# Copies of x to the output: issued one by one inside the experts' tiles instead of all ahead of the first expert weights

## The chip, the cores and the metric

The kernel runs as one program on one core of a Trainium2 chip. The metric is the device time of one execution in microseconds (us), lower is better. The time before is 1151.77 us, the median of 3 runs (1147.62 to 1153.18). The core has five engines, each with an instruction queue of its own that it works off strictly in order: PE (TensorE, matrix products), DVE (VectorE, elementwise and reductions), ACT (ScalarE, functions and copies), POOL (GpSimd, here mostly issuing indirect transfers) and SP (SyncE, issuing DMA transfers). Transfers run on 16 DMA engines that all issuers share.

## The reference

```python
xn = layernorm(x)                          # x: 8 x 512 x 256, f32
# recurrent attention, 16 heads of 16, for each token:
S = S * exp(gk)[..., None]
sab = einsum('bhk,bhkv->bhv', a, S)
S = S + k[..., None] * (sab[..., None, :] + v[..., None, :])
o_t = einsum('bhk,bhkv->bhv', q, S)
s = layernorm(o * sigmoid(xn @ Wog1 @ Wog2)) * norm_w @ Wo
# mixture of experts, 8 experts, the best 2 for each token:
for e in range(8):
    moe += cw[:, e] * (gelu(xn @ W1[e] + b1[e]) @ W2[e] + b2[e])
out = x + s * silu(layernorm(moe) * gamma + beta)
```

x has 4096 tokens of 256 numbers, W1 of an expert is 256 x 1024 and W2 1024 x 256, so that the weights of one expert are 2 MB.

## The kernel before

**Stages and chunks.** The 512 steps of a sequence are cut into 8 stages of 64 steps. Within a stage the recurrence is solved in closed form over chunks (of 16 or 8 steps, in turns by stage), so that the state S is renewed 48 times in all: chunks c0 to c47. The chain of chunks is the serial backbone. In a chunk PE first multiplies the state with the stage's tables (`by_state`, matmul L898), DVE makes `RO` of it (L929), PE multiplies `RO` with the keys `KT` (`by_keys`, L963), ACT decays the state (L908), and DVE renews it (`S`, L975). The tables FA and KT of a stage are made ahead by `fine(s)` and `solve`, which are long runs of DVE work (lines 713 to 816); `output` (L1026, L1035) makes the stage's output, also on DVE. `fetch(s)` (L651) loads a stage's projected queries, keys and decays from memory as `raw` (L654), and `turn_keys` has ACT copy them to `X` (L666), with which the stage's DVE work begins.

**Experts.** `experts` works through 39 tiles of sorted token rows, t0 to t38: 32 tiles of 256 rows (two pieces of 128) and 7 half tiles of 128 rows, 71 pieces in all. For a tile, `load_weights` (L1063 to L1069) issues 2 transfers of 1 MB on SP (w1 at L1066, w2 at L1068), one tile ahead; `load_rows` gathers rows on POOL (L1078); `turn` transposes them (L1091). PE then makes `ph` (L1122, 16 matmuls, in four groups, each followed by a Gelu on ACT, L1130), and `py` (L1143, 8 matmuls for a piece); ACT scales it to `y` (L1151), and POOL adds it to the sums in memory by an indirect transfer (`y_dram`, L1099). The trace records each of these matmuls twice, so 16 matmuls are 32 records.

**Attention's end and the finish.** For each stage, `attend(s)` loads `by_state` and `o_f` on SP, adds them (DVE, L1206), gates them with a sigmoid of `p2` (PE L1213, ACT L1217, DVE L1220), takes moments (L1164) and normalizes (ACT, L1177), transposes on PE (`pz`, L1234), and multiplies with Wo (`po`, L1241). The buffers behind `by_state`, the gate and the transposed copy are one and the same, single (tag `t_f`), and so is `o_f`, so that the stages follow one another here. When the last tile is done, `fetch_sums` reads the sums of all stages back on POOL (L1268), and `finish(s)` takes moments of them (DVE, L1164), normalizes, applies gamma, beta and SiLU, multiplies with the attention's part, and adds the product to the output in memory (an accumulating transfer on POOL). The output must hold x by then: 16 copies of 256 KB (8 stages x 2 halves, L1370) move it there from memory to memory, issued on SP by `everything_else` just before `experts` starts, in build order. `behind(instruction, now["spread"])` only pins such an instruction's place behind another one in the schedule.

**What sets the order.** The program is built by generators that `yield` estimated costs. `stretch(s)` goes through the chunks of a stage, and at set points of each chunk `both` spends credit on three lists: `inner` (the DVE work of `recurrence`), `between` (`attend`) and `beside` (sorting, projections, `experts`, `finish`). What `beside` gets at a chunk is `per_chunk` = (`beside_cost` - what is spent) / (chunks left + 4), so `beside_cost` (L1428) sets how soon the experts' tiles are placed among the chunks. The tiles that are left when the chunks are over come after them, mixed with the last stages of `attend`. Each engine then runs its instructions in the order in which they were so placed.

Of the kernel before, what the change touches and what calls it, by code (L numbers as in the profile page):

```python
# [30 lines left out]
def recurrent_attn_moe_kernel(  # L31
# [23 lines left out]
    nc = tc.nc  # L55
# [5 lines left out]
    NF = DFF // P  # L61
    NTB = T // NB
    NP = B * NB // P
# [15 lines left out]
    def bank(name):  # L79
        return ps_p.tile([P, 512], F32, tag="ps", name=name)  # L80
# [61 lines left out]
    for i in range(2):  # L142
        t = sp.tile([P, GC, 2 * D], F32, name=f"vz{i}", bufs=1)
# [5 lines left out]
    def rows_of(ap, s, bb):  # L149

        return ap.rearrange("(c bb) t d -> bb t c d", bb=2)[bb, s * NB : (s + 1) * NB]

    made, now = {}, {}
# [484 lines left out]
    def behind(ins, first):  # L638

        tc.add_manual_dep(  # L640
            ins.ins,
            first.ins.name,
            mybir.DependencyInfo(mybir.DependencyClass.NoSync, mybir.DependencyReason.DATA),
            reason="what it waits for has that long",
        )
# [416 lines left out]
    def experts(mp):  # L1062
        def load_weights(t):  # L1063
            e = nc.sync.value_load(owner[0:1, t : t + 1], min_val=0, max_val=E - 1)
            w1 = mp.tile([P, KD, DFF], F32, name="w1")
            nc.sync.dma_start(w1, W1[bass.ds(e, 1)].rearrange("o (j p) f -> p (o j) f", p=P))  # L1066
            w2 = mp.tile([P, NF, D], F32, name="w2")
            nc.sync.dma_start(w2, W2[bass.ds(e, 1)].rearrange("o (f p) d -> p (o f) d", p=P))  # L1068
            return w1, w2  # L1069

        def pieces(t):

            return range(2 * t, 2 * t + 2) if t < NXW else (NXW + t,)

        def load_rows(t):
            xs = mp.tile([P, TS // P, D], F32, name="xs", bufs=4)
            for n, r in enumerate(pieces(t)):
                nc.gpsimd.indirect_dma_start(  # L1078
                    out=xs[:, n],
                    out_offset=None,  # L1080
                    in_=xn_dram[:, :],
                    in_offset=bass.IndirectOffsetOnAxis(ap=source[:, r : r + 1], axis=0),
                )
            return xs

        def turn(t, xs):
            size = len(pieces(t))
            pt = bank("pt").rearrange("p (j t) -> p j t", j=KD)
            for j in range(KD):
                for n in range(size):  # L1090
                    nc.tensor.transpose(  # L1091
                        pt[:, j, n * P : (n + 1) * P], xs[:, n, j * P : (j + 1) * P], ident
                    )
            xT = mp.tile([P, KD, TS], F32, name="xT_s")
            nc.scalar.copy(xT[:, :, : size * P], pt[:, :, : size * P])
            return xT

        def add_to_sums(r, y):
            nc.gpsimd.indirect_dma_start(  # L1099
                out=y_dram[:, :],  # L1100
                out_offset=bass.IndirectOffsetOnAxis(
                    ap=target[:, r : r + 1], axis=0
                ),
                in_=y,
                in_offset=None,
                compute_op=ALU.add,
            )

        now_xs, nxt = load_rows(0), load_rows(1)
        w1, w2 = load_weights(0)  # L1110
        xT = turn(0, now_xs)
        yield 0.9
        for t in range(NX):
            size = len(pieces(t)) * P
            hs = []
            for f in range(0, NF, 2):
                ph = bank("ph").rearrange("p (k t) -> p k t", k=2)
                h = mp.tile([P, 2, TS], F32, name="h", bufs=6)
                hs.append(h)
                for k in range(2):  # L1120
                    for j in range(KD):
                        nc.tensor.matmul(  # L1122
                            ph[:, k, :size],
                            w1[:, j, (f + k) * P : (f + k + 1) * P],
                            xT[:, j, :size],
                            start=(j == 0),
                            stop=(j == KD - 1),
                        )
                for k in range(2):
                    nc.scalar.activation(  # L1130
                        h[:, k, :size], ph[:, k, :size], AF.Gelu, bias=bias[:, t, f + k : f + k + 1]
                    )
                if f == 0:
                    now_xs, nxt = nxt, load_rows(t + 2) if t + 2 < NX else None
                    ahead = load_weights(t + 1) if t + 1 < NX else None
                yield 1.9
            if t + 1 < NX:
                xT = turn(t + 1, now_xs)
                yield 0.9
            for n, r in enumerate(pieces(t)):  # L1140
                py = bank("py")[:, :D]
                for f in range(NF):
                    nc.tensor.matmul(  # L1143
                        py,
                        hs[f // 2][:, f % 2, n * P : (n + 1) * P],
                        w2[:, f],
                        start=(f == 0),
                        stop=(f == NF - 1),
                    )
                y = mp.tile([P, D], F32, name="y", bufs=4)  # L1150
                nc.scalar.activation(y, py, AF.Identity, scale=weight[:, r : r + 1])  # L1151
                add_to_sums(r, y)
                if n == 0 and size == TS:
                    yield 3.9
            if ahead:
                w1, w2 = ahead
            yield 3.9

    experts_cost = NXW * (4 * 1.9 + 0.9 + 2 * 3.9) + NXH * (4 * 1.9 + 0.9 + 3.9)
# [106 lines left out]
    def fetch_sums(fp, s):  # L1266
        g = fp.tile([P, NP, D], F32, name="g", bufs=NTB)
        nc.gpsimd.dma_start(  # L1268
            g,
            y_dram[s * NP * P : (s + 1) * NP * P].rearrange("(n p) d -> p n d", p=P),  # L1270
        )
        return g

    def finish(fp, s, g):
        mv = fp.tile([P, NP, 2], F32, name="mv_g", bufs=4)
        for i in range(NP):
            moments(fp, g[:, i], i, mv)
        yield 2.5
        r = yield from deviation(fp, mv)
        for i in range(NP):  # L1280
            normed(g[:, i], i, r)
        yield 1.0
        wide = [P, NP, D]
        nc.vector.tensor_tensor(g, g, now["gam"].unsqueeze(1).to_broadcast(wide), ALU.mult)
        yield 1.2
        nc.vector.tensor_tensor(g, g, now["bet"].unsqueeze(1).to_broadcast(wide), ALU.add)
        nc.scalar.activation(g, g, AF.Silu)
        yield 1.2
        if s in LATE:
            gated[s] = g  # L1290
            return
        while s not in attended:
            yield WAIT
        att = fp.tile([P, NP, D], F32, name="att_f", bufs=3)
        nc.gpsimd.dma_start(att, att_d[s].rearrange("n p d -> p n d"))
        yield 1.0
        nc.vector.tensor_tensor(g, g, att, ALU.mult)  # L1297
        yield 1.2
        for bb in range(2):
            nc.gpsimd.dma_start(  # L1300
                rows_of(out, s, bb), g[bb * NB : (bb + 1) * NB], accum_op=ALU.add
            )
# [56 lines left out]
    def everything_else():  # L1359

        for s in range(2, NTB):
            yield from project(s, xT_all[:, s])
        while not cp:
            yield WAIT
        projecting.close()
        prologue.close()

        for s in range(NTB):
            for bb in range(2):
                behind(nc.sync.dma_start(rows_of(out, s, bb), rows_of(x, s, bb)), now["spread"])  # L1370
            yield 0.2
        with tc.tile_pool(name="moe", bufs=2, side="right") as mp:
            yield from experts(mp)
        fp = late.enter_context(tc.tile_pool(name="fin", bufs=2, side="right"))
        for name, ap in (("gam", gamma), ("bet", beta)):
            now[name] = fp.tile([P, D], F32, name=f"{name}_sb", bufs=1)
            nc.sync.dma_start(now[name], ap.partition_broadcast(P))
        sums = [fetch_sums(fp, s) for s in range(NTB)]
        yield 1.0
        for s in range(NTB):  # L1380
            beside.queue.append(finish(fp, s, sums[s]))
# [43 lines left out]
        cost = fine_cost(s + 1) if s + 1 < NTB else 0.0  # L1425
        return cost + output_cost(s - 1) if s else cost

    beside_cost = experts_cost + (NTB - 2) * NP * 2 * 1.8 + 16 * 0.8 + 8 * 0.5 + 64 * 0.7 + 10 + NTB * 0.4  # L1428

    def stretch(s):  # L1430
        C = CS[s]
# [84 lines left out]
```

## Time and profile before

| what | value |
|---|---|
| median of 3 runs | 1151.77 us |
| profiled execution | 1149.24 us, of which the span 1147.4 us |
| mean granted TensorE clock | 0.883 |
| PE busy | 894.6 us (78%) |
| DVE busy | 878.1 us (77%) |
| ACT busy | 688.0 us (60%) |
| POOL busy | 355.6 us (31%) |
| memory traffic | 196 GB/s over the span |

No engine is busy all the time, and the shares are means over very different stretches. Until about 250 us the kernel projects, sorts and prepares; from there to about 1010 us it works through the chunks with the experts' tiles among them; then come the tiles that are left, and the finish.

How rows of the timeline are read: start (us from the start of the span), time, engine, line, operation, tiles (written <- read), shape, number of records; in brackets the time that the engine stood idle before, and the releaser that ended it.

### The profile page before, as it was taken

The numbers are of one execution on the slowest core, as the hardware profiler recorded it, in microseconds if no ns is written. First come the engines' busy times: TensorE is split into PE (matmuls) and PEld (weight loads), VectorE is DVE, ScalarE is ACT, GpSimd is POOL, SyncE is SP. The second block draws the span as 40 slices with busy tenths as digits, with TensorE's granted clock in tenths as the row PEclk, the third lists the DMA queues.
The fourth block names the chain that finished last, engine by engine and source line by source line (L and its number), as shares of the span: only waits on it lengthen the run. The fifth ranks groups of instructions, "written<-read, shape, count | busy, mean of one in ns | idle before, by whom it ended". The sixth has DMA issues, their size and how long they took to land. (4 is left out here: it accounts for less than half of the span.)

```text
span 1147.4 us, 24978 instructions
## 1 busy us (share of the span) xinstructions
PE 894.6 (78%) x9448; PEld 684.9 (60%) x9448; DVE 878.1 (77%) x1761; ACT 688.0 (60%) x1687; POOL 355.6 (31%) x312
## 2 busy tenths in 40 slices
PE   5979778619989869978899798679799889785312
PEld 2534354417778658856687577568587667684301
DVE  7579995959999695579999975999999546313494
ACT  3566566854456847665658478248765645434385
POOL 2300000132344323323446323244642134220334
PEclk9989888958999989998899889789899989997666
DMA  8777578689578976997499899477599987894786
GB/s 224 190 177 194 147 213 135 184 290 217 170 165 252 180 221 143 259 221 187 120 278 137 252 170 241 141 159 247 176 191 225 182 201 226 143 241 126 225 182 103
DMA packets 393255, 221.87 MB, mean 193 GB/s; under 512 B 280912, under 2 KB 362704, under 8 KB 392112
## 3 DMA queue, kind: packets, MB, share of 16 engines
q1 hardware_dynamic: 363248, 172.17, 60.6%
q0 software_dynamic: 25280, 43.93, 18.3%
q10 hardware_dynamic: 4608, 4.20, 1.5%
q8 instruction: 74, 1.21, 0.4%
q14 instruction: 45, 0.37, 0.1%
HBM read 152.07 MB, written 72.35 MB: 196 GB/s over the span
## 5 line engine op out<-in xcount | busy, mean ns | idle before, releaser
L1122 PE MATMUL ph<-xT_s,w 128*128 128x256 f32 (+1 forms) x1248 | 291.0, 390 | 16.3 <-DMA w<-in_L_ffn_W_dram 9.0
L1143 PE MATMUL py<-w,h 128*128 128x256 f32 x1136 | 275.8, 398 | 8.6 <-ACT h L1130 8.1
L1122 PEld LDWEIGHTS ph<-xT_s,w 128*128 128x128 f32 x1248 | 234.6, 206 | 53.1 <-issue 11.0
L1143 PEld LDWEIGHTS py<-w,h 128*128 128x128 f32 x1136 | 221.0, 200 | 46.0 <-ACT h L1130 12.9
L908 ACT ACTIVATE sdec<-S,PcF 128x64 f32<-128x64 f32 x752 | 189.6, 340 | 90.9 <-DVE S L975 82.0
L1099 POOL DMA_INDIRECT y_dram<-y,target x71 | 139.2, 1960 | 291.6 <-ACT y L1151 149.3
L1078 POOL DMA_INDIRECT xs<-xn_dram,source x71 | 116.9, 1646 | 343.1 <-DVE source L536 169.7
L1130 ACT ACTIVATE h<-ph,bias 128x256 f32<-128x256 f32 (+1 forms) x312 | 121.4, 450 | 79.6 <-PE ph L1122 78.6
L975 DVE SCALAR_TENSOR_TENSOR S<-PC,heads,sdec 128x256 f32<-128x256 f32 x188 | 78.9, 481 | 51.6 <-PE PC L963 43.4
L1151 ACT ACTIVATE y<-py,weight 128x256 f32<-128x256 f32 x71 | 33.1, 468 | 90.0 <-PE py L1143 89.9
L898 PE MATMUL PC<-S,FA 64*16 64x64 f32 (+1 forms) x3072 | 43.5, 234 | 50.2 <-DVE S L975 49.9
L963 PE MATMUL PC<-RO,KT 8*64 8x64 f32 (+1 forms) x3008 | 49.3, 242 | 35.8 <-DVE RO L929 20.8
L963 PEld LDWEIGHTS PC<-RO,KT 8*64 8x64 f32 (+1 forms) x3008 | 41.1, 139 | 55.2 <-DVE RO L929 25.5
L898 PEld LDWEIGHTS PC<-S,FA 64*16 64x16 f32 (+1 forms) x3072 | 34.3, 100 | 65.5 <-DVE S L975 55.6
L808 DVE TENSOR_TENSOR scratch_a<-Z,A 128x1020 f32<-128x1020 f32 (+21 forms) x88 | 67.8, 771 | 5.3 <-ACT fq L772 4.4
L733 DVE TENSOR_TENSOR scratch_q<-Z,X 128x64 f32<-128x64 f32 (+11 forms) x96 | 70.5, 734 | 0.0
L746 DVE TENSOR_REDUCE Z<-scratch_q 128x4 f32<-128x64 f32 (+11 forms) x96 | 70.1, 730 | 0.0
L816 DVE TENSOR_TENSOR Z<-Z,scratch_a 128x1020 f32<-128x1020 f32 (+21 forms) x88 | 67.6, 768 | 1.0
L1234 PE MATMUL pz<-ident,o_f 128*128 128x128 f32 x64 | 13.0, 334 | 61.9 <-ACT o_f L1177 61.4
L750 DVE TENSOR_TENSOR Z<-Z,X 128x64 f32<-128x64 f32 (+10 forms) x88 | 60.6, 688 | 0.1
L733 DVE TENSOR_TENSOR scratch_a<-Z,X 128x64 f32<-128x64 f32 (+10 forms) x88 | 60.5, 688 | 0.0
L746 DVE TENSOR_REDUCE A<-scratch_a 128x4 f32<-128x64 f32 (+10 forms) x88 | 60.3, 685 | 0.0
(227 smaller groups left out, 1366.0 us busy)
## 6 DMA issues: line engine op xcount, KB each, us to landing
w<-in_L_ffn_W_dram SPq DMA_DIRECT2D x78, 1024.0 KB
kqd<-st_p SPq DMA_DIRECT2D x48, 256.0 KB
raw<-kqd SPq DMA_DIRECT2D x8, 1536.0 KB
fq<-fq SPq DMA_DIRECT2D x8, 1024.0 KB
xn_dram<-xn SPq DMA_DIRECT2D x8, 512.0 KB
v<-st_p ACTq DMA_DIRECT2D x32, 128.0 KB
y_dram<-st_b SPq DMA_DIRECT2D x16, 256.0 KB
kt<-Z SPq DMA_DIRECT2D x8, 512.0 KB
```

The lines of the kernel that those rows point to most:

```text
L733: nc.vector.tensor_tensor(pr, Z[:, :, :upto, C:], step[:, m, i].unsqueeze(2).to_broadcast([P, n, upto, HD]), ALU.mult,)
L746: now["work"] = nc.vector.tensor_reduce(to, pr, AX.X, ALU.add)
L808: nc.vector.tensor_tensor(pr, Z[:, :, l, l:].unsqueeze(2).to_broadcast([P, n, l, w]), A[:, :, l, :l].unsqueeze(3).to_broadcast([P, n, l, w ...
L898: nc.tensor.matmul(p1[32 * q : 32 * q + 2 * C, b, m], FA[lo : lo + SB, 4 * q + m, c], S[lo : lo + SB, q, m], start=True, stop=True,)
L908: nc.scalar.activation(dec[:, n // 4, n % 4], S[:, n // 4, n % 4], AF.Copy, scale=PcF[:, n, c : c + 1])
L963: nc.tensor.matmul(p4[b * SB : (b + 1) * SB, q, m], KT[32 * q : 32 * q + C, lo : lo + SB], ro[32 * q : 32 * q + C, lo : lo + SB], start=Tr ...
L975: nc.vector.scalar_tensor_tensor(S.rearrange(flat)[:, :, at], p4.rearrange(flat)[:, :, at], heads[:, h : h + 1], now["dec"].rearrange(flat ...
L1078: nc.gpsimd.indirect_dma_start(out=xs[:, n], out_offset=None, in_=xn_dram[:, :], in_offset=bass.IndirectOffsetOnAxis(ap=source[:, r : r + ...
L1099: nc.gpsimd.indirect_dma_start(out=y_dram[:, :], out_offset=bass.IndirectOffsetOnAxis(ap=target[:, r : r + 1], axis=0), in_=y, in_offset=None,
L1122: nc.tensor.matmul(ph[:, k, :size], w1[:, j, (f + k) * P : (f + k + 1) * P], xT[:, j, :size], start=(j == 0), stop=(j == KD - 1),)
L1130: nc.scalar.activation(h[:, k, :size], ph[:, k, :size], AF.Gelu, bias=bias[:, t, f + k : f + k + 1])
L1143: nc.tensor.matmul(py, hs[f // 2][:, f % 2, n * P : (n + 1) * P], w2[:, f], start=(f == 0), stop=(f == NF - 1),)
```

## The change

The 16 copies are no longer issued together ahead of `experts`, but in the loop over a tile's groups: at the third of the four `ph` groups of the odd tiles t = 1, 3, ... 31, one copy each on SP, without `behind`. The planner's cost `beside_cost` is altered too: its second term was (8 - 2) x 4 x 2 x 1.8 = 86.4 and is now (8 - 2) x 7 x 1.8 = 75.6, and the last term, 8 x 0.4 = 3.2, is gone; so 769.6 became 755.6, of which the experts' own cost is 608.4.

```diff
--- before.py
+++ after.py
@@ -1130,6 +1130,10 @@
                     nc.scalar.activation(
                         h[:, k, :size], ph[:, k, :size], AF.Gelu, bias=bias[:, t, f + k : f + k + 1]
                     )
+                if f == NF // 2 and t % 2 and t // 2 < 2 * NTB:
+
+                    copy = t // 2 // 2, t // 2 % 2
+                    nc.sync.dma_start(rows_of(out, *copy), rows_of(x, *copy))
                 if f == 0:
                     now_xs, nxt = nxt, load_rows(t + 2) if t + 2 < NX else None
                     ahead = load_weights(t + 1) if t + 1 < NX else None
@@ -1364,11 +1368,6 @@
             yield WAIT
         projecting.close()
         prologue.close()
-
-        for s in range(NTB):
-            for bb in range(2):
-                behind(nc.sync.dma_start(rows_of(out, s, bb), rows_of(x, s, bb)), now["spread"])
-            yield 0.2
         with tc.tile_pool(name="moe", bufs=2, side="right") as mp:
             yield from experts(mp)
         fp = late.enter_context(tc.tile_pool(name="fin", bufs=2, side="right"))
@@ -1425,7 +1424,7 @@
         cost = fine_cost(s + 1) if s + 1 < NTB else 0.0
         return cost + output_cost(s - 1) if s else cost
 
-    beside_cost = experts_cost + (NTB - 2) * NP * 2 * 1.8 + 16 * 0.8 + 8 * 0.5 + 64 * 0.7 + 10 + NTB * 0.4
+    beside_cost = experts_cost + (NTB - 2) * 7 * 1.8 + 16 * 0.8 + 8 * 0.5 + 64 * 0.7 + 10
 
     def stretch(s):
         C = CS[s]
```

## The prediction

> **What bounds the kernel now.** I read three views of the profile: busy time by stretches, then the timeline around the first weights, where the change acts, then the timeline of the tail. The stretches first (length, busy time of PE, PE's weight loads, DVE, ACT and POOL, then granted clock, share of the DMA engines, GB/s):
>
> ```profile
> 245.00:440.00 195.00, 162.20 (x2129) 133.82 (x2130) 175.83 (x297) 113.70 (x305) 61.96 (x54) 0.90 0.82 202
> 440.00:500.00 60.00, 55.39 (x676) 46.32 (x676) 26.39 (x55) 44.50 (x110) 19.53 (x17) 0.98 1.02 209
> 500.00:640.00 140.00, 125.03 (x1609) 102.16 (x1608) 138.18 (x246) 89.50 (x239) 65.42 (x42) 0.91 0.77 187
> ...
> 900.00:1010.00 110.00, 89.50 (x1327) 74.72 (x1326) 53.33 (x136) 54.07 (x185) 35.96 (x27) 0.91 0.91 190
> 1010.00:1082.00 72.00, 42.82 (x243) 36.72 (x241) 15.48 (x52) 28.21 (x59) 16.85 (x19) 0.80 0.67 168
> 1082.00:1148.00 66.00, 15.25 (x56) 10.94 (x56) 46.56 (x120) 42.44 (x70) 24.34 (x25) 0.60 0.78 167
> ```
>
> See the DVE column: 175.83 of 195 us at 245 to 440 and 138.18 of 140 at 500 to 640, above PE's 162.20 and 125.03; so the stage work of DVE sets the pace there and PE has room. At 440 to 500 and 900 to 1010 it is PE. From 1010 on nobody is full: that is a chain of waits. Now the start:
>
> ```profile
> 209.37 8.61 SPq L1370 DMA_DIRECT2D out_dram<-in_L_attn_x_dram  x9
> ...
> 233.08 1.54 SPq L654 DMA_DIRECT2D raw<-kqd  x1
> ...
> 237.48 12.02 SPq L1370 DMA_DIRECT2D out_dram<-in_L_attn_x_dram  x7
> ...
> 245.48 5.62 ACT L666 COPY X<-raw 128x1024 f32<-128x1024 f32 x3 [10.12 <-DMA raw<-kqd]
> 245.69 1.18 PE L963 MATMUL PC<-RO,KT 16*64 16x64 f32 x52 [8.19 <-DMA KT<-kt]
> 249.29 0.20 DVE L713 COPY dec<-X 128x64 f32<-128x64 f32 x1 [10.69 <-ACT X L666]
> 249.72 0.43 SPq L1066 DMA_DIRECT2D w<-in_L_ffn_W_dram  x1
> ...
> 258.96 8.67 PE L1122 MATMUL ph<-xT_s,w 128*128 128x256 f32 x32
> ```
>
> Seven of the copies keep SP until 249.5 us, and the first weights go out at 249.72. PE has little from 237 to 259. But `ph` has no bracket: when PE reached it, straight behind chunk 1's L963, the weights were there; not they, but its place in PE's order kept it. The tail:
>
> ```profile
> 1060.08 2.84 PE L1122 MATMUL ph<-xT_s,w 128*128 128x128 f32 x24
> ...
> 1063.91 3.72 PE L1143 MATMUL py<-w,h 128*128 128x256 f32 x16
> ...
> 1068.42 1.58 POOL L1099 DMA_INDIRECT y_dram<-y,target  x1 [6.37 <-DMA by_state<-ro]
> 1073.25 1.23 DVE L1206 TENSOR_TENSOR o_f<-o_f,by_state 128x1024 f32<-128x1024 f32 x1 [21.62 <-DMA og<-og]
> 1074.24 1.63 POOL L1268 DMA_DIRECT2D g<-y_dram  x2 [4.23 <-DMA y_dram<-y,target]
> ...
> 1082.26 0.75 DVE L1164 BATCH_NORM_STATS2 st_f<-g 128x6 f32<-128x256 f32 x2 [3.62 <-DMA g<-y_dram]
> ...
> 1085.08 2.17 PE L1234 MATMUL pz<-ident,o_f 128*128 128x128 f32 x8 [17.44 <-ACT o_f L1177]
> ```
>
> The last tile's `py` ends at 1067.6, its scatter starts at 1068.42, the sums are read back from 1074.24, DVE has them at 1082.26, and the finish takes 1147.4 - 1082.26 = 65.1 us more. Stage 6 of `attend` (L1206 at 1073.25, `pz` at 1085.08) lies beside this and keeps nobody.
>
> **The change, part by part.** (1) The copies. In the order of the changed build, 7 still stand on SP ahead of the first weights (they depend on nothing and nothing holds them), among the last projections' stores; 9 come at later tiles. Issue: nine at 8.61/9 = 0.96 us at most, 8.6 us of SP spread over some 500 us, where SP only runs ahead. As bytes: 9 x 256 KB = 2.36 MB, read and written, at the page's mean 193 GB/s 12.2 us of a moved load whose total is the same, at stretches where the DMA share is 0.77 to 1.02. Behind each copy on SP stand the weights of a later tile, and KT loads. Bounds 0 and +12; I take +1, because a tile's weights go out a whole tile ahead.
>
> (2) The first weights go out ahead of `raw` and the KT loads of stage 0, at about 217 (where the nine copies' issue ended, 209.37 + 8.61 = 218.0). Tile 0 then stands on PE between chunk 0's L898 and L963, and tile 1 begins at chunk 1. A whole tile is 2 x (291.0 + 275.8)/71 = 16.0 us of PE, from the costly groups' busy times over 71 pieces. Most of it falls in PE's hole (8.19 us at 245.69 alone, 8.16 more ahead of chunk 1). Bounds for the chain: -16, if the tile is carried through as time, and +4, if it stands in front of chunk 0's L963. In favour of nothing: the renewals from 253 to 446 are paced by DVE (first row). I added, for each span between two renewals, the DVE work and the PE work that each build places in it, by these durations. From c0 to c12 the larger one sums to 186.4 us before and 181.0 after (192.9 real), from c12 to c16 63.1 and 64.5, c16 to c24 125.2 and 121.9, c24 to c29 97.6 and 94.0, c29 to c38 136.2 and 142.8, c38 to c46 91.9 and 95.5; in all 700.4 and 699.7. What PE gains early it gives back from c29 on. So the last renewal moves by -0.7; real time is 751.7, so 51.3 us are waits of other kinds, and I put +-7 on it.
>
> (3) `raw` of stage 2. It reached ACT 12.4 us after its issue (233.08 to 245.48), with seven copies right behind it; the other stages' took 7.1 to 19.3. Without the copies it can come 5.3 us sooner, or, behind 3 MB of weights now ahead of it, 6.9 later. DVE's idle 10.69 us ends there. Bounds -5.3 and +6.9; I take 0.
>
> The Trainium skill bears on (2) and (3) ("DMA: Bandwidth & Descriptors", section "Queues, rings and completion order"): on each DMA engine the descriptors of one issuer's ring are taken in order. By it the first weights would stand behind every copy that was issued before them, and taking nine away would free them by the 12.2 us that was worked out above. By the row, `ph` at 258.96 waits for no weights. By the rule taken as time, my total would be 12 us less, 1161; I follow the row. Against any gain speaks the same page's section "Issuing engines are not separate DMA queues": all transfers share 16 engines, so that a copy moved is still carried.
>
> (4) The planner. 14.0 less in `beside_cost` lowers `per_chunk` in each chunk, so that the experts fall behind. In the build's order, 35.5 tiles of `ph` and 67 pieces of `py` stand ahead of c47 before, and 34.5 and 66 after: one half tile more in the tail. That alone is 32 `ph` records at 2.84/24 us, 3.8, and 16 `py` records, 3.72: +7.5 us.
>
> (5) But the tail's order changes with it. `attend` is placed on its own credit, and so slides by one half tile against the experts. Before, stage 6's transposes `pz` stand behind the last tile. After, PE's order at the last tile is: 4 `ph` matmuls, half of `pz` of stage 6, 8 `ph`, the other half, 4 `po`, 4 `ph`, 8 `py`. So 12 of the 16 `ph` and all `py` of the last tile queue behind a wait for stage 6 to be normalized. Its L1206 starts at 1073.25, on transfers issued on SP when stage 5 freed `t_f`, which nothing here moves. From there by the rows: the gate product at 1075.63 takes 1.22, the moments end at 1078.64, the root (0.30) at 1078.97, reciprocal and bias (0.14 + 0.16) at 1079.3, the first two normalizations (half of 2.08) at 1080.3. Then on PE two halves of `pz` (2.17), 24 `ph` records (2.84), a `po` group with its copy (about 0.5 + 0.7), a Gelu pair (0.62) and `py` (3.72): 10.5 us, end at 1090.8 where before it was 1067.6. That is +23.2. Sums, scatter, read-back and finish hang on it unchanged: the scatter at about 1091.6, DVE's first moments at 1105.5. Lower bound, were stage 6 ready: +7.5. Upper: +27, with two more table loads on ACT (1.28 each) between Gelu and roots and a slower `zT` copy. The finish may win 0 to 3 us, since stage 6's roots and transposes no longer lie in it; -1.
>
> Sum against the profiled 1149.24: +1 (copies) -0.7 (chain) +0 (`raw`) +23.2 (tail, half tile included) -1 = +22.5, so 1171.7. The median of the runs stood 2.5 above the profiled run; half of that taken, 1173.
>
> **Rivals.** R1: the tile that starts early is carried as time, and the tail loses all the same: 1173 - 16, or -12 to -18: 1155 to 1161. For it: 51 us of waits beyond the two engines' work, and ends at c39 to c41 where PE sets the pace. Against: DVE's 175.83 of 195.
>
> R2, the other side: the slide opens no wait. If stage 6's L1206 is not late at the last tile (its transfers freed earlier because stage 5's `po` comes one half tile earlier on PE), the tail costs only +7.5, and with the early tile's -16 and `raw`'s -5.3 it comes to 1151.8 - 13.8 = 1138, without the latter two to 1159. It decides from the point where `pz` of stage 6 is ready before about 1068 + 5. For: `by_state` of stage 6 goes out only when stage 5's buffer is free, at 1060. Against: stage 5's own `pz` at 1053.69 waits for ACT, not for PE, so it does not move with the tiles.
>
> R3: the spread copies meet the weights in stretches where the DMA share is near 1 (1.02 at 440 to 500): +12 on top, 1185, and with KT loads late, up to 1200.
>
> R4: the change does little of what it says, since 7 copies stay ahead: then (2) and (3) shrink, but (4) and (5) do not; the time stays in the forecast's range.
>
> **How the numbers follow.** Forecast with R4 0.66, R1 0.12, R2 0.14, R3 0.08. The predicted time is the forecast's, 1173, with its own range 1165 to 1181 (the chain's 7 and the tail's +4 and -3). The range of 8 in 10 reaches down into R1 and up to R3's lower end: 1156 to 1187. What a measurement here can tell from no change is 0.5%, 5.8 us: R2 gives 0.11 faster and 0.03 same, R1 0.03 same and 0.09 slower; so faster 0.11, same 0.06, slower 0.83.
>
> **What would show it.** Right, if `pz` of stage 6 precedes the last `ph` and `py` with a long wait on ACT's L1177, the last scatter starts near 1091 and DVE's first moments of the sums near 1105; if the renewal of c46 stays within 7 us of 1004.9, while the first weights go out at about 217. Wrong, if the renewals run 12 us or more ahead (R1, R2), if `pz` of stage 6 starts below 1075 (R2), or if KT or weights end PE's waits in mid-run (R3).

## The result and the profile after

The changed kernel is slower: 1161.88 us (median of 16 runs, 1153.42 to 1168.84) against 1149.45 us for the kernel before in the same rounds (16 runs, 1143.18 to 1156.19). The ratio is 1.0102, with a 95% interval of 1.008 to 1.0124. The profiled execution has a span of 1162.9 us, 15.5 more than that of before. Ratios, here and below, leave out four slow runs of the kernel before, so that they differ a little from the quotient of the medians.

I cut both profiled executions at the same events: the first DVE instruction (L975) that renews the state for chunk 0 (c0), 2, 12, 29 and 46, the start of the last scatter on POOL, and the end. These stretches, in us, carry the whole account:

| stretch | before | after | difference |
|---|---|---|---|
| start to c0 | 253.2 | 252.9 | -0.3 |
| c0 to c2 | 44.8 | 30.0 | -14.8 |
| c2 to c12 | 148.1 | 146.0 | -2.1 |
| c12 to c29 | 300.8 | 299.4 | -1.4 |
| c29 to c46 | 258.0 | 268.8 | +10.8 |
| c46 to the last scatter | 63.5 | 86.8 | +23.3 |
| last scatter to the end | 79.0 | 78.9 | -0.1 |

So three things happened: the chain of chunks gained 17 us by c12 and had kept that by c29, it gave 11 back by c46 (so that c46 comes 7.7 us earlier than before), and the tail lost 23. First the beginning, the timeline of the changed kernel (start, time, engine, line, operation, tiles, shape, records, and in brackets the idle time with its releaser):

```profile
217.86 0.41 SPq L1066 DMA_DIRECT2D w<-in_L_ffn_W_dram  x1
...
235.50 7.66 PE L1122 MATMUL ph<-xT_s,w 128*128 128x256 f32 x32
...
243.09 0.36 PE L963 MATMUL PC<-RO,KT 16*64 16x64 f32 x12
...
243.87 5.34 PE L1147 MATMUL py<-w,h 128*128 128x256 f32 x24
...
249.14 0.81 PE L963 MATMUL PC<-RO,KT 16*64 16x64 f32 x52
...
251.76 0.20 DVE L713 COPY dec<-X 128x64 f32<-128x64 f32 x1 [12.30 <-ACT X L666]
...
256.75 1.06 PE L898 MATMUL PC<-S,FA 64*32 64x64 f32 x64 [3.14 <-DVE S L975]
```

The first weights go out at 217.86, not at 249.72, and most of tile 0 (32 records of `ph`, 24 of `py`) now stands on PE before chunk 0's keys are through (L963, 12 records ahead of `py` and 52 behind it). But c0 itself is not earlier. The windows from c0 to c2 and from c2 to c12 (length; busy time of PE, its weight loads, DVE, ACT, POOL; clock, DMA share, GB/s), with the row of chunk 2's `RO`, before and then after:

```profile
253.20:298.00 44.80, 37.92 (x398) 31.54 (x399) 44.77 (x88) 18.40 (x56) 12.05 (x9) 0.86 0.80 193
...
291.61 0.69 DVE L929 TENSOR_TENSOR RO<-PC,vz 128x512 f32<-128x512 f32 x1
...
298.00:446.00 148.00, 129.10 (x1767) 106.36 (x1766) 132.04 (x209) 92.91 (x258) 51.53 (x46) 0.93 0.82 199
```

```profile
252.90:282.90 30.00, 26.19 (x357) 21.66 (x356) 29.02 (x70) 19.83 (x56) 8.46 (x7) 0.94 0.58 140
...
276.01 0.68 DVE L929 TENSOR_TENSOR RO<-PC,vz 128x512 f32<-128x512 f32 x1
...
282.90:428.90 146.00, 120.44 (x1731) 98.28 (x1729) 144.49 (x232) 90.86 (x249) 64.20 (x45) 0.94 0.79 199
```

From c0 to c2 DVE was full in both kernels, 44.77 of 44.80 us and 29.02 of 30.00: in the builds with the early tile, chunk 2's `RO` stands further ahead in DVE's queue, before 15.8 us of a stage's preparation, and runs 15.6 us earlier. From c2 to c12 DVE made up for most of it, 12.5 us more work in 2 us less time: before it was idle for 16 us there, after for 1.5. That is why the gain was kept. The largest single idle time of before, 5.92 us, ends with stage 3's `X`, which ACT copies from `raw`; the timeline of before, then of after:

```profile
365.05 3.92 SPq L654 DMA_DIRECT2D raw<-kqd  x1
...
380.65 0.23 DVE L713 COPY dec<-X 128x128 f32<-128x128 f32 x1 [5.92 <-ACT X L666]
```

```profile
343.94 3.30 SPq L654 DMA_DIRECT2D raw<-kqd  x1
...
374.84 0.28 DVE L713 COPY dec<-X 128x128 f32<-128x128 f32 x1
```

SP works in order, and its weight loads wait for PE to free a buffer: from 298 to 446 us of before, 33 us of SP's waits at L1066 and L1068 ended with PE's `ph` and `py`. SP comes to `raw` 21 us sooner, and DVE no longer waits for it (no bracket). That PE's earlier tiles are what brings SP there sooner fits these rows but was not tested alone, and of the other 10 us of DVE's idle time the waits name only ACT (3.8 and 2.0 us). Now the tail of the changed kernel:

```profile
1065.60 1.23 DVE L1210 TENSOR_TENSOR o_f<-o_f,by_state 128x1024 f32<-128x1024 f32 x1 [22.22 <-DMA og<-og]
...
1072.46 1.18 PE L1238 MATMUL pz<-ident,o_f 128*128 128x128 f32 x4 [11.48 <-ACT o_f L1181]
...
1073.44 3.26 PE L1122 MATMUL ph<-xT_s,w 128*128 128x128 f32 x16
...
1079.60 3.62 PE L1147 MATMUL py<-w,h 128*128 128x256 f32 x16
...
1084.00 1.54 POOL L1099 DMA_INDIRECT y_dram<-y,target  x1 [21.56 <-ACT y L1155]
...
1097.07 0.75 DVE L1168 BATCH_NORM_STATS2 st_f<-g 128x6 f32<-128x256 f32 x2 [25.34 <-DMA g<-y_dram]
```

The transposes of stage 6 stand in front of most of the last expert tile, PE waits 11.48 us for them to become possible, and the scatter, the read-back and the finish hang on that tile. DVE has its first moments of the sums 14.8 us later than at 1082.26.

### The profile page after: what moved, and what is told of

It reads as the page before. It is cut to its first block, busy times and chain, and to the rows that moved or that the text cites. A ratio compares the mean times of both kernels' runs of the same rounds, so it can differ in the third digit from the quotient of the medians.

```text
span 1162.9 us, 24983 instructions
## 1 busy us (share of the span) xinstructions
PE 888.6 (76%) x9448; PEld 681.3 (59%) x9448; DVE 873.0 (75%) x1761; ACT 698.6 (60%) x1692; POOL 369.6 (32%) x312
## 4 chain that ended last, share of the span: by engine, by line
DVE 34%; PE 24%; DMA 18%; ACT 9%; issue 6%; SPq 6%; POOL 2%; ACTq 1%; DVEq 0%; POOLq 0%
PE ph L1122 8%; PE py L1147 7%; DMA w<-in_L_ffn_W_dram 4%; DVE scratch_q L733 4%; DVE Z L746 3%; DVE A L746 3%; DVE Z L750 3%; DVE S L975 3%; DVE scratch_a L733 3%; DVE O L1035 2%; DVE Z L816 2%; DVE scratch_o L1026 2%; PE pp L261 2%; ACT X L666 2%; DVE scratch_a L808 2%
## 5 line engine op out<-in xcount | busy, mean ns | idle before, releaser
L1147 PE MATMUL py<-w,h 128*128 128x256 f32 x1136 | 270.0, 392 | 13.5 <-ACT h L1130 13.5
L1099 POOL DMA_INDIRECT y_dram<-y,target x71 | 166.9, 2351 | 294.2 <-ACT y L1155 161.5
L1147 PEld LDWEIGHTS py<-w,h 128*128 128x128 f32 x1136 | 216.3, 196 | 47.0 <-ACT h L1130 16.1
L1078 POOL DMA_INDIRECT xs<-xn_dram,source x71 | 103.0, 1451 | 347.3 <-DMA w<-in_L_ffn_W_dram 169.0
L975 DVE SCALAR_TENSOR_TENSOR S<-PC,heads,sdec 128x256 f32<-128x256 f32 x188 | 78.9, 475 | 41.2 <-PE PC L963 30.4
L898 PE MATMUL PC<-S,FA 64*16 64x64 f32 (+1 forms) x3072 | 44.0, 236 | 53.3 <-DVE S L975 53.2
L898 PEld LDWEIGHTS PC<-S,FA 64*16 64x16 f32 (+1 forms) x3072 | 34.7, 101 | 69.3 <-DVE S L975 62.1
L963 PE MATMUL PC<-RO,KT 8*64 8x64 f32 (+1 forms) x3008 | 49.9, 242 | 29.7 <-DVE RO L929 25.3
L1238 PE MATMUL pz<-ident,o_f 128*128 128x128 f32 x64 | 12.7, 321 | 77.3 <-ACT o_f L1181 77.1
L963 PEld LDWEIGHTS PC<-RO,KT 8*64 8x64 f32 (+1 forms) x3008 | 41.2, 139 | 49.6 <-DVE RO L929 32.7
```

Source lines behind the costliest of these rows:

```text
L963: nc.tensor.matmul(p4[b * SB : (b + 1) * SB, q, m], KT[32 * q : 32 * q + C, lo : lo + SB], ro[32 * q : 32 * q + C, lo : lo + SB], start=Tr ...
L975: nc.vector.scalar_tensor_tensor(S.rearrange(flat)[:, :, at], p4.rearrange(flat)[:, :, at], heads[:, h : h + 1], now["dec"].rearrange(flat ...
L1078: nc.gpsimd.indirect_dma_start(out=xs[:, n], out_offset=None, in_=xn_dram[:, :], in_offset=bass.IndirectOffsetOnAxis(ap=source[:, r : r + ...
L1099: nc.gpsimd.indirect_dma_start(out=y_dram[:, :], out_offset=bass.IndirectOffsetOnAxis(ap=target[:, r : r + 1], axis=0), in_=y, in_offset=None,
L1147: nc.tensor.matmul(py, hs[f // 2][:, f % 2, n * P : (n + 1) * P], w2[:, f], start=(f == 0), stop=(f == NF - 1),)
```

## The experiments

All times are medians of runs on the same chip as runs of the kernel before; a ratio stands against these. Stretches come from one profiled execution each; c2 to c46 took 708.8 to 716.2 us in the four that share the changed kernel's order up to there, so that a few us of a stretch prove little.

**First theory: early tile and late tail are two effects, of the copies' move and of the planner's cost.** Copies moved, with the old cost:

```diff
-    beside_cost = experts_cost + (NTB - 2) * 7 * 1.8 + 16 * 0.8 + 8 * 0.5 + 64 * 0.7 + 10
+    beside_cost = experts_cost + (NTB - 2) * NP * 2 * 1.8 + 16 * 0.8 + 8 * 0.5 + 64 * 0.7 + 10 + NTB * 0.4
```

> The changed kernel with the old beside_cost of 769.6, so that the copies alone are moved. In its build tile 0 still begins in PE's early hole, and the tail's order on PE is that of before (pz of stage 6 behind the last py). Theory 1 (early tile gains in the chain, the planner's cost loses in the tail): renewal of c12 at 428 to 432 us against 446.1 before, last scatter 8 to 16 us earlier than 1068.4, time 1134 to 1143, faster than both. Rival (the planner's smaller share makes the early chunks faster): c12 at 443 to 449, time 1146 to 1153.

Measured: 1158.54 us, ratio 1.0061 (1.0028 to 1.0094): a miss. c0 to c2 took 30.0, c46 to the last scatter 64.6: both as expected. But c12 came at 437.6 (c0 4.4 us later than before), c29 to c46 took 266.9, the finish 4.2 us more, and the time is worse than before. And the planner's cost alone, in the kernel before (the opposite edit on the other kernel):

> The kernel before with the new beside_cost of 755.6, copies as before. Its build has tile 0 behind chunk 1 on PE as before, and pz of stage 6 ahead of the last ph and py. Theory 1: renewal of c12 at 443 to 449, pz of stage 6 with a wait of 8 us or more on ACT, last scatter 15 to 24 us later than before, time 1165 to 1174, slower than the changed kernel. Rival (the planner makes the early chunks faster): c12 at 428 to 434, time 1158 to 1164 like the changed kernel.

Measured: 1168.19 us, ratio 1.0133 (1.0086 to 1.0179). c0 to c2 is 44.8 as before, c29 to c46 256.8, c46 to the last scatter 88.7. So the early tile belongs to the copies' move, the 23 to 25 us of the tail to the planner's cost alone. Its tail shows the same row:

```profile
1078.42 1.18 PE L1234 MATMUL pz<-ident,o_f 128*128 128x128 f32 x4 [11.37 <-ACT o_f L1177]
...
1090.14 1.54 POOL L1099 DMA_INDIRECT y_dram<-y,target  x1 [21.61 <-ACT y L1151]
```

**The tail's wait.** On the changed kernel, with a list `done` that is filled when the experts are all placed:

```diff
             normed(o[:, i], i, r)
         yield 1.0
+        while s == NTB - 2 and not done:
+            yield WAIT
         zT = pool.tile([P, NP, KD, P], F32, tag="t_f", name="zT", bufs=1)
```

> The changed kernel, with pz of stage 6 held in the build until the experts are all placed, so that it stands behind the last py on PE; everything ahead of it as in the changed kernel. Theory 1: the 11.5 us wait and the transposes leave the last tile's path, last scatter at about 1068 to 1071 instead of 1084, time 12 to 16 us less than the changed kernel: 1146 to 1150. Rival (the tail is late because the last tile itself is late, one half tile and its weights): 1157 to 1162, last scatter 1078 or later.

Measured: 1161.47 us, ratio 1.0094 (1.006 to 1.0127): a miss. From c46 to the last scatter it took 77.1, not the 71 to 74 that the expected scatter stands for. Its timeline at the last tile shows why:

```profile
1074.44 1.23 DVE L1211 TENSOR_TENSOR o_f<-o_f,by_state 128x1024 f32<-128x1024 f32 x1 [22.27 <-DMA og<-og]
...
1075.70 1.08 ACT L1222 ACTIVATE sg<-p 128x512 f32<-128x512 f32 x2 [2.06 <-DVE o_f L1211]
...
1076.35 6.33 PE L1148 MATMUL py<-w,h 128*128 128x256 f32 x16 [3.78 <-ACT sg L1222]
...
1083.46 1.54 POOL L1100 DMA_INDIRECT y_dram<-y,target  x1 [12.21 <-ACT y L1156]
```

With PE's order mended, ACT's queue held the same wait: the sigmoid of stage 6 stands ahead of the last Gelus, and starts only after DVE's L1211, which reads the buffer that the sigmoid writes, and which waits for a transfer. So the hold was moved ahead of all of stage 6 that computes:

```diff
+        while s == NTB - 2 and not done:
+            yield WAIT
         behind(nc.vector.tensor_tensor(o, o, t, ALU.add), now["work"])
```

> The changed kernel with all of stage 6 of attend from its first addition on (L1210) held in the build until the experts are placed, so that neither PE's transposes nor ACT's sigmoid of stage 6 stand ahead of the last tile. Theory 2 (the last tile is late because it queues behind stage 6, on ACT as well as on PE): last scatter 69 to 73 us after c46, against 86.8 in the changed kernel, 77.1 with pz alone moved and 63.5 before; time 1146 to 1153. Rival (the last tile is late by itself): 77 us or more, time 1157 to 1162.

Measured: 1152.41 us against 1154.91, ratio 0.9997 (0.997 to 1.0024). From c46 to the last scatter it took 69.9:

```profile
1063.31 3.73 PE L1123 MATMUL ph<-xT_s,w 128*128 128x128 f32 x32
...
1066.88 3.62 PE L1148 MATMUL py<-w,h 128*128 128x256 f32 x16
...
1070.08 1.22 DVE L1213 TENSOR_TENSOR o_f<-o_f,by_state 128x1024 f32<-128x1024 f32 x1 [23.04 <-DMA o_f<-o]
...
1071.28 1.54 POOL L1100 DMA_INDIRECT y_dram<-y,target  x1 [5.47 <-ACT y L1156]
```

The last tile runs through without waiting for DVE's L1213. Of the 23.3 us, 16.9 were the wait (86.8 to 69.9); 6.4 are left (69.9 against 63.5), about what the half tile more would cost.

**What gives back 11 us between c29 and c46.** The changed kernel without its copies:

> The changed kernel without the 16 copies: x is left out of the output. Theory 1 (spread copies cost next to nothing): 1158 to 1163 us, c12 at 426 to 431, c42 at 940 to 945. Rival (the spread copies collide with weights and KT loads from c28 on, and this is what gives back the chain's gain): c42 at 928 to 934, time 1146 to 1152.

Measured: 1157.42 us, ratio 1.0045 (1.0013 to 1.0077). c29 to c46 took 257.7 against 268.8, so the difference is tied to the copies; c42 at 933.4 lies in the rival's range, the time just below the first theory's and above the rival's. The medians differ by less than the stretches, 4.5 us: without the copies c0 came 6.1 us later, and the finish took 2.6 more. Next, one copy in each of the tiles 0 to 15, with the new and with the old cost:

```diff
-                if f == NF // 2 and t % 2 and t // 2 < 2 * NTB:
-                    copy = t // 2 // 2, t // 2 % 2
+                if f == NF // 2 and t < 2 * NTB:
+                    copy = t // 2, t % 2
```

> The changed kernel with one copy in each of the tiles 0 to 15 instead of the odd ones up to 31, so that no copy is left beside the last third of the chain; planner and order of the tail as in the changed kernel. Theory 2 (the tile that begins early takes 15 us off c0 to c2, the late tail adds 23 us, and copies beside c29 to c46 add 10): c0 to c2 30 us, c29 to c46 257 to 261 us against 268.8, time 1150 to 1157. Rival (the 10 us there belong to the tiles' order or to a draw of the run, not to the copies): c29 to c46 266 to 270, time 1159 to 1164.

Measured: 1170.46 us, ratio 1.015 (1.0103 to 1.0196): c29 to c46 256.4, about as the theory had it, but c12 to c29 307.7 in place of 299.4, and the time missed. The loss seemed to go with the copies, which now lay at 406 to 593 us.

> One copy in each of the tiles 0 to 15, and the old beside_cost: the early tile without copies beside the end of the chain and with the tail's order of before. Theory 2: c0 to c2 30 us, c29 to c46 257 to 261, c46 to the last scatter 63 to 66, time 1134 to 1142, faster than the kernel before. Rival (where PE sets the pace at the end the early gain is given back, copies or not, as in the run with the copies alone): c29 to c46 265 to 269, time 1149 to 1158.

Measured: 1161.61 us, ratio 1.0064 (1.0033 to 1.0095): c12 to c29 307.9, c29 to c46 260.1, c46 to the scatter 63.9. A miss. And the copies together, as before, but not pinned:

```diff
-                behind(nc.sync.dma_start(rows_of(out, s, bb), rows_of(x, s, bb)), now["spread"])
+                nc.sync.dma_start(rows_of(out, s, bb), rows_of(x, s, bb))
```

> The kernel before with the 16 copies still together ahead of the experts but not pinned behind the spread; in its build 1.0 tile of ph and no py stands between chunks 0 and 1 (1.25 and 2 in the changed kernel). Theory 2: c0 to c2 is 35 to 42 us (44.8 before, 30.0 after), a part of that is kept, time 1140 to 1148. Rival (only copies inside the tiles let a tile into the hole): c0 to c2 43 to 46, time 1147 to 1154.

Measured: 1158.86 us, ratio 1.0053 (1.0023 to 1.0083). c0 to c2 took 30.8, better than expected, but c2 to c12 155.7, c12 to c29 306.0 and c29 to c46 263.7: the gain was lost with no copy beside a chunk. That speaks against the copies as such. Then each copy twice, the second of a pair for another stage:

> The changed kernel with two copies where it issues one, the second of the pair for another stage, so that each part of x is copied twice; 22 copies instead of 9 then lie beside the chunks. Theory 3 (a copy beside the chunks costs its transfer, 1.3 to 1.8 us each, wherever it lies): 13 more cost 17 to 23 us, c12 to c46 584 to 592 us against 568 in the changed kernel, time 1176 to 1186. Rival (copies cost nothing in themselves; what differs between the runs is a draw): c12 to c46 566 to 572, time 1159 to 1165.

Measured: 1179.18 us, ratio 1.0241 (1.0191 to 1.0291); c12 to c46 576.8. The time fits the theory, the stretch falls between the two. The changed kernel again, in the same rounds:

> The changed kernel once more, on the same chip as the two others, to see how far its stretches differ from one profiled execution to the next. All theories: c0 253 to 260, c0 to c2 30, c2 to c46 711 to 717, c46 to the last scatter 86 to 88, time 1158 to 1165.

Measured: 1161.6 us, ratio 1.008 (1.0048 to 1.0112), c12 to c46 563.2, c2 to c46 708.8, c46 to the scatter 88.5, c29 to c46 264.8. So c2 to c46 moved by 5 us from one execution to the next, and what c29 to c46 gave back is 7 to 11 us. Then who issues: the copies from ACT, each pinned behind a Gelu, so that all 16 lie beside tiles.

```diff
-                    nc.sync.dma_start(rows_of(out, *copy), rows_of(x, *copy))
+                    behind(nc.scalar.dma_start(rows_of(out, *copy), rows_of(x, *copy)), gelu)
```

> The changed kernel with the copies issued from ACT, each pinned behind the last Gelu of its group, so that all 16 lie beside the odd tiles and none in SP's queue. Theory 3a (what a copy costs is its transfer on the DMA engines, whoever issues it): c12 to c46 572 to 582 us, c2 to c46 719 to 729, time 1166 to 1176. Rival 3b (it is SP's queue: weights and KT loads wait behind the copy's turn): c12 to c46 550 to 557, c2 to c46 697 to 705, time 1150 to 1158, as without copies.

Measured: 1156.09 us, ratio 1.0046 (1.0015 to 1.0078); c12 to c46 556.2, c2 to c46 705.3. Theory 3a falls: 16 transfers beside the chunks cost at most some 7 us (698.1 without copies). Next, the same 16 pinned copies from SP, and then a quarter of each, in a build whose order on PE, DVE, ACT and SP is the same, instruction by instruction:

```diff
-behind(nc.sync.dma_start(rows_of(out, *copy), rows_of(x, *copy)), gelu)
+behind(nc.sync.dma_start(rows_of(out, *copy)[:, :1], rows_of(x, *copy)[:, :1]), gelu)
```

> The run with 16 copies pinned beside the odd tiles, but issued from SP as in the changed kernel (from ACT it took 705.3 us from c2 to c46, without copies 698.2, and the changed kernel with 9 copies on SP 714.2 and 708.9). Theory 4 (the bytes of a copy in SP's queue hold up what stands behind them there): c2 to c46 717 to 727 us, time 1164 to 1173. Rival (what differs is the place of the chunks' work in the build, not the copy): 703 to 712, time 1154 to 1160.

Measured: 1172.74 us, ratio 1.0141 (1.0099 to 1.0182), c2 to c46 716.4: the time in theory 4's range, the stretch just below it.

> The same with a quarter of each copy, 64 KB in place of 256, and the same order on every engine: three quarters of x are left out of the output. Theory 4 (bytes): c2 to c46 701 to 708 us, 10 to 20 less than with whole copies, time 1152 to 1160. Rival a (the instruction in SP's queue and its wait for a free lane cost, whatever its size) and rival b (the build's order costs): within 4 us of the run with whole copies.

Measured: 1175.13 us, ratio 1.017 (1.0132 to 1.0208), c2 to c46 713.3. With three quarters of the bytes gone the time is the same, where theory 4 had 1152 to 1160. So it is not the bytes. Theory 4 falls, and what is left is rival a (the instruction's place in SP's queue) or rival b (the order of the build).

Single chunks show where the orders differ. The time from one renewal to the next, in us (without copies and with 16 on ACT, PE's order is the same; the four runs of the changed kernel's order differ in the tail alone; the last two share theirs):

```
chunk            c26    c30    c34    c38    c42
before           13.2   18.2   19.4   13.0   17.7
no copies        11.5   15.8   18.7   19.1   13.2
16 on ACT        11.8   15.8   19.8   19.0   13.2
changed          15.4   19.1   26.3   24.0   15.8
changed again    15.4   19.1   25.6   24.0   15.8
pz held          15.4   19.1   26.3   24.0   15.8
stage 6 held     15.4   19.1   25.6   24.0   15.8
16 on SP         14.3   18.0   24.0   23.6   15.4
quarter on SP    14.3   18.0   23.4   23.6   15.4
```

In these five chunks the times come back to within 1.1 us, mostly 0.1, where the order is the same. They are not the loss itself: the changed kernel has 22.3 us more in them than the one without copies, and other chunks between c26 and c46 give some 8 back. What such a difference is can be read at c34, by the stretch between the two renewals, first without copies, then of the changed kernel, each with the renewal at its end:

```profile
806.18:824.88 18.70, 18.28 (x202) 15.01 (x201) 16.44 (x44) 16.34 (x36) 9.38 (x8) 0.97 1.19 131
...
824.88 1.26 DVE L975 SCALAR_TENSOR_TENSOR S<-PC,heads,sdec 128x256 f32<-128x256 f32 x3
```

```profile
804.38:830.67 26.29, 19.89 (x203) 16.09 (x202) 23.41 (x59) 18.44 (x37) 7.79 (x8) 0.87 0.97 127
...
830.67 1.65 DVE L975 SCALAR_TENSOR_TENSOR S<-PC,heads,sdec 128x256 f32<-128x256 f32 x4
```

Neither renewal waits for anything: in the changed kernel DVE has 15 more instructions ahead of it, 7.0 us of the 7.6. ACT's order differs there too:

```profile
813.89 0.84 ACT L1130 ACTIVATE h<-ph,bias 128x256 f32<-128x256 f32 x2
...
816.79 1.89 PE L1241 MATMUL po<-wo_sb,zT 128*128 128x256 f32 x8
```

```profile
811.44 3.91 ACT L908 ACTIVATE sdec<-S,PcF 128x64 f32<-128x64 f32 x16
...
818.23 0.84 ACT L1130 ACTIVATE h<-ph,bias 128x256 f32<-128x256 f32 x2
...
819.12 3.78 PE L1245 MATMUL po<-wo_sb,zT 128*128 128x256 f32 x8 [5.54 <-ACT h L1130]
```

Without copies ACT does the first Gelus of the tile between the ninth and the tenth of the 16 decays, and PE goes on to `po` without a wait. In the changed kernel these Gelus stand behind all 16 decays and two table loads, and PE stands 5.54 us until they have freed the buffer that `po` writes (`ph`, `py`, `pz` and `po` share four). This wait does not set the renewal of c34's end, which DVE's queue holds until 830.67. The next copy of x (L1136) goes out only at 830.38. So a copy on SP changes the neighbours' places in the build, and the loss shows in how the new places fit: from c29 to c46 DVE's work is the same (192.79 us without copies, 193.33 in the changed kernel, 193.35 in its second profile), and what grew is its idle time. By the releasers, its waits ended with ACT for 13.3, 19.7 and 19.0 us, with PE for 31.0, 33.0 and 31.5, with a transfer for 19.4, 21.3 and 19.3. Most of the growth is ACT's, little a transfer's. That the order is all of the 7 to 11 us is not shown, and neither is which single place costs what. Rival a stays open: SP took 23.6 us over its 16 whole copies, 18.5 over the 16 quarters, and ACT 9.6 over its 16.

**A version from the terms.** Stage 6 held, and the copies two by two in the last eight tiles:

```diff
-                if f == NF // 2 and t % 2 and t // 2 < 2 * NTB:
-                    copy = t // 2 // 2, t // 2 % 2
-                    nc.sync.dma_start(rows_of(out, *copy), rows_of(x, *copy))
+                if f == NF // 2 and t >= NX - NTB:
+                    for bb in range(2):
+                        copy = t - (NX - NTB), bb
+                        nc.sync.dma_start(rows_of(out, *copy), rows_of(x, *copy))
```

> The changed kernel with stage 6 held until the experts are placed, and the copies issued two by two in the last eight tiles, so that nearly all lie behind the last chunk, where the share of the DMA engines was 0.54. Theory 3: c0 to c46 726 to 734 us against 741 to 746 with nine copies beside the chunks, c46 to the last scatter 69 to 76, time 1140 to 1149, faster than the kernel before. Rival (the copies delay the tail's loads by as much as they freed the chunks of): c46 to the last scatter 80 or more, time 1151 to 1160.

Measured: 1138.83 us against 1152.05, ratio 0.9877 (0.9831 to 0.9924): faster than both kernels, and by more than expected. One copy went out at 215 us, five from 937 to 977 beside the last chunks, ten later. c0 to c46 took 728.4, c46 to the last scatter 78.1, between the theory and the rival, some 8 more than with stage 6 held alone. The range came from theory 3, the copies' transfer, which the runs with ACT's copies and with quarter copies refuted afterwards; c12 to c46 took 552.4, as without copies (552.1), so its chain is that of the run without copies. The other place, all copies from ACT, unpinned, which puts them at the kernel's start:

> Stage 6 held until the experts are placed, and the copies issued from ACT without a pin, which puts all 16 within the first instructions of the kernel. Expected from the sum (early tile, no copies beside the chunks, tail without the wait): c2 to c46 696 to 704 us, c46 to the last scatter 69 to 73, time 1136 to 1146, unless the copies hold up the first loads of x: then c0 is 5 us or more later than the 249 to 260 seen so far.

Measured: 1148.61 us against 1155.16, ratio 0.9943 (0.9914 to 0.9971). c2 to c46 698.9, c46 to the scatter 68.7, as expected; but c0 is at 265.8 us, the risk that was named: PE's first transposes of x start at 22.82 us, at 14.13 with stage 6 held alone. It beats the kernel before by less.

## Why the prediction was right or wrong

The direction was right, the size was not: the sum was +22.5 us against the profiled execution of before; the profiled executions differ by 15.5 and the medians by 12.4. Of the 7.0 us between the sum and the profiles, the chain with copies and `raw` makes 8.0 (+0.3 in the sum, -7.7 measured at c46), and the finish takes 1 back.

**Part 5, the tail, was right in mechanism and size.** The forecast +23.2 for the last tile is +23.3 from c46 to the last scatter, with the order of PE and the long wait on ACT that it named. The bound for the half tile alone, +7.5, compares with 6.4 in the run with stage 6 held. The forecast of the scatter at 1091 and of the moments at 1105 missed by 7 to 8 us because the chain ran ahead by that much. What the prediction had not seen is that ACT's queue held the same wait a second time; with `pz` alone moved the time stayed at 1161.47 us.

**Part 2, the early tile, is the step that failed: "the last renewal moves by -0.7".** It was worked out from the larger of DVE's and PE's work for each span between renewals, with the 51.3 us of waits beyond that taken as fixed to within 7. Summed by stretch, it had -5.4 from c0 to c12, -5.5 from c12 to c29 and +10.2 from c29 to c46; the runs show -16.9, -1.4 and +10.8. The step that failed is the first: from c0 to c12 DVE's work fell by only 3.3 us (176.81 to 173.51), and 13.6 us came out of the waits that were taken as fixed (DVE's idle time, 16.1 to 2.5 us). The largest of them, 5.9 us, had ended with stage 3's `raw`. The +10.2 came near the measured value by luck: it stood for more work of PE, but PE was busy for 221.71 us from c29 to c46 before and for 216.59 after, and the run without copies, with 218.22, took 257.7 like the kernel before. The prediction's own sign of being wrong, renewals 12 us or more ahead, came true at c12 (17.2) and c29 (18.6). Rival R1, which carried the early tile as time, had this half right: its price of 16 us is near what was gained by c12, but only 7.7 of it was left at c46.

**Part 1, the copies: "I take +1" with bounds of 0 and +12.** The count was right (7 ahead of the first weights, 9 from 583 to 956 us). From c29 to c46 the changed kernel took 11.1 us more than the run without copies, 7.1 in its second profile, so the upper bound was near; but with a quarter of the bytes, on which this bound rested, 16 copies on SP took the same time as with all. The builds with copies on SP have another order around them, and DVE's added waits end mostly with ACT. So R3 had nearly the number, and hardly the mechanism. Its sign, waits of PE for weights, is there in part: 8.3 us from c29 to c46, against 3.4 before and 3.1 without copies, and up to these 5 us may be R3's.

**Part 3, `raw` of stage 2,** was taken as 0: DVE's L713 came at 251.76 in place of 249.29, within the bounds. The `raw` that mattered was the one of the next stage.

**Part 4** was right: the planner's change alone, in the kernel before, makes the tail of the changed kernel.

The two rules that the prediction weighed come out differently. By the Trainium skill ("DMA: Bandwidth & Descriptors", section "Issuing engines are not separate DMA queues") all transfers share the same DMA engines whoever issues them. With the same 16 copies from ACT or from SP the runs took 1156.09 and 1172.74 us, which that rule does not explain, and a quarter of the bytes changed nothing, so here the bytes were not what was paid. From the section "Queues, rings and completion order" the prediction had worked out, as an estimate, that the first weights would be free 12 us earlier. SP issued them 32 us earlier, since they no longer stood behind KT loads and `raw` either, and the gain at c2 was 14.8.

That a tile's early start alone is kept is not general: with the copies together and unpinned it was there (30.8) and was lost by c29. Why that build loses it, and whether the plain place of an instruction in SP's queue costs something besides the order, stays open.

## What to carry to other kernels

Idle time of an engine that sets the pace is not a fixed cost: ask what ended it, and whether that comes from the very work that is moved. Where a planner places work by costs, a small edit moves the order of everything after it: compare the two builds' orders on each engine, look for a wait that now stands ahead of the work that ends last, and look on every queue that serves that work, since mending one may leave the same wait on another. To price a moved transfer, shrink its bytes with the order kept: if the time stays, it was not the bytes, and the order around the transfer is the next suspect.

## What was not expected of the hardware

With one and the same instruction order, chunk times came back to 0.1 us in many places (c26 15.4, c30 19.1, c38 24.0 in four executions), while c0 lay between 250.9 and 260.1 us in these four. Part of that is a stretch of PE that one execution has and another has not. In the changed kernel chunk 0's 64 records of L898 took 1.36 us; in the run with `pz` held, whose order is the same there, 44 of them took 1.28 us and the other 20 some 6 us more, in small groups, each behind an idle time that nothing in the profile explains ("issue"):

```profile
233.27 1.28 PE L898 MATMUL PC<-S,FA 64*32 64x64 f32 x44
...
234.86 0.40 PE L898 MATMUL PC<-S,FA 64*32 64x64 f32 x3 [0.31 <-issue]
...
235.60 0.44 PE L898 MATMUL PC<-S,FA 64*32 64x64 f32 x4 [0.34 <-issue]
...
236.38 0.29 PE L898 MATMUL PC<-S,FA 64*32 64x64 f32 x1 [0.34 <-issue]
```

c0 came at 260.1 us there and at 252.9 in the changed kernel. The runs do not show what PE waited for.
